# Moving the exponentials one turn later and the squares amid the next unit's scores, in a fused attention and spectral kernel

## The chip, the cores and the metric

The kernel runs on one core of a Trainium2 chip. The core has five engines that work in parallel, each through its own stream of instructions and in order: TensorE (PE, matrix products; its weight loads are listed apart as PEld), VectorE (DVE), ScalarE (ACT), GpSimd (POOL), and SyncE (SP), which here issues the transfers (DMAs). Matrix products read from the on-chip memory SBUF and write to PSUM, which has eight banks of 128 partitions by 512 float32. The metric is the device time of one execution in microseconds, the median of several runs.

## The reference

Two layers, each with a residual, on x of shape (2, 48, 48, 768), all in float32:

```python
qkv = (x.reshape(B, S, dim) @ qkv_w + qkv_b).reshape(B, S, 3, nh, hd)   # S = 2304, 12 heads of 64
...
attn = jnp.einsum('bqc,bkc->bqk', q * scale, k)
rel_h = jnp.einsum('bhwc,hkc->bhwk', r_q, Rh)
rel_w = jnp.einsum('bhwc,wkc->bhwk', r_q, Rw)
attn = (attn.reshape(B * nh, h, w, h, w) + rel_h[:, :, :, :, None] + rel_w[:, :, :, None, :]).reshape(B * nh, S, S)
attn = jax.nn.softmax(attn, axis=-1)
out = (attn @ v).reshape(B, nh, h, w, hd)
...
x = x + attention(_gn(x)) @ proj_w + proj_b
x = x + spectral(_gn(x))    # rfft2, two block-diagonal layers of 8 blocks, softshrink, irfft2
```

`_gn` is a group norm over 32 groups. The change lies in the attention alone; the output projection and the spectral layer stay as they are.

## The kernel before

The two images of the batch are done one after the other: attention, output projection, spectral layer. The normalized input stands transposed in SBUF (`xnT`, channels on the partitions). Attention goes through the heads in 6 pairs, a pair through 6 groups of 8 image rows (384 queries), a group through 3 units of 128 queries (x = 0, 1, 2). So there are 108 units for each image, `order[n]` = (pair, group, x), and one pass of the loop over n (line 502) is a turn.

The work on one unit of two heads:

- `new_unit` (L346): POOL adds the unit's two relative terms from `rhw` into `s`, two operations of 128 x 2304. `s` has four buffers.
- `scores` (L360): ten PE products, five pieces of keys by two heads, into the PSUM banks `ps_s`; DVE adds each to `s` and takes its maximum into `mx`; one reduction makes `nm`, the negated maximum.
- `numerators` (L389): four ACT exponentials, in place in `s`, two halves by two heads, with the sums in `parts`.
- `squares` (L403): DVE transposes `s` in 32 x 32 squares, in place, two operations for each half.
- `exchange` (L409): moves the squares between partitions into `pT`, so that keys stand on the partitions: for each half two ACT copies and six transfers on SP's queue. `pT` has two buffers.
- `weigh` (L423): 36 pairs of PE products of `pT` with the values, into the one bank `ps_o`.
- `finish` (L440): ACT copies `ps_o` to `res`, DVE adds up `parts` into `dens`; after x = 2 SP writes `res` to DRAM (`oT`). `inverses` (L458) takes the reciprocal of six units' sums, which PE transposes (`turn`) and SP writes to `inv_d` in three transfers (`send`).

Beside the units, a turn has one piece of projection work that fills PE: with x = 2 the queries of the group after next (`queries`), otherwise one sixth of the next pair's keys or values (`keys`, `values`). The last pair has no next one, so only its queries are left there. In turns with x = 0, `relative` (L295) multiplies the queries of a group with the table of relative positions; ACT copies the two banks `ps_r` to `rel`, `write` sends `rel` to a DRAM scratch `t` in a skewed layout (two transfers), and `read` fetches the terms from there into `rhw` (two transfers; a read must wait until its write has landed). `load_w` (L194) loads a weight block for the next pair; keys and values share one buffer.

The order of each engine is the order in which the code emits its instructions: PE, DVE, ACT and SP are wrapped in `InOrder`. Evictions of projection banks are put into the lists `by_act` and `by_dve` and emitted by `evict` at a fixed place in the turn. The PSUM banks other than `ps_o` are seven, handed out in turn to `ps_s`, `ps_proj`, `ps_v`, `ps_r` and `ps_i`, so a product waits until the bank seven places earlier has been emptied.

A turn emits, for unit n (`un`), n-1 (`last`) and n-2 (`older`), in this order: scores(un), numerators(un), projection work and weight loads, turn, weigh(older), relative, the ACT evictions, squares and exchange of half 1 of last, write, squares and exchange of half 0 of un, the DVE evictions, read, finish(older), new_unit for n+1, send. In the last turns of an image the functions of `Projection` are called too (`late`): `step` loads the projection weights and the first attention outputs and inverses, and `fill` emits the first output products.

Of the kernel before, what the change touches and what calls it, by code (L numbers as in the profile page):

```python
# [17 lines left out]
P = 128  # L18
# [144 lines left out]
def attention(tc, k, x_b, a, oT, inv_d, late, span, ps_b, ps_o):  # L163
# [12 lines left out]
    with ExitStack() as ctx:  # L176
# [65 lines left out]
        def evict(waiting):  # L242
            while waiting:
                waiting.pop(0)()
# [50 lines left out]
        def relative(g, qT):  # L295

            row0 = min(32, 40 - 8 * g)  # L300
            both = [bank(f"ps_r{h}") for h in range(2)]
            for x in range(3):
                for h in range(2):
                    r = slice(h * HD, (h + 1) * HD)
                    rows = k.rel[r, row0 : row0 + RW]
                    step = REL + 32 - 16 * x - row0
                    pe.matmul(
                        both[h][:, x * 2 * RW : (x + 1) * 2 * RW],
                        lhsT=qT[r, x, :],
                        rhs=bass.AP(rows.tensor, rows.offset, [rows.ap[0], [step, 2], [1, RW]]),  # L310
                        start=True,
                        stop=True,
                    )
            for h in range(2):
                dst = rel[:, :, :, h, :].rearrange("p k x j -> p x k j")
                src = both[h][:, :ROW].rearrange("p (x k j) -> p x k j", x=3, k=2)
                by_act.append(lambda dst=dst, src=src: act.copy(dst, src))

            rhw = qp.tile([P, 3, 2, 2 * HW], F32, tag="rhw", name="rhw")
            t_ds = []  # L320

            def write():
                for kind in range(2):
                    t_d = dp.tile([P * RS + 16], F32, tag=f"t{kind}", name=f"t{kind}")
                    t_ds.append(t_d)
# [17 lines left out]

            return rhw, write, read
# [11 lines left out]
            return {"pr": pr, "g": g, "x": x, "qT": qT, "s": s}  # L356

        PIECES = [(k0, min(S, k0 + 512)) for k0 in range(0, S, 512)]

        def scores(un):  # L360

            mx = smallp.tile([P, 2, len(PIECES)], F32, tag="mx", name="mx")
            for j, (k0, k1) in enumerate(PIECES):
                both = [bank(f"ps_s{h}") for h in range(2)]
                for h in range(2):
                    r = slice(h * HD, (h + 1) * HD)
                    pe.matmul(
                        both[h][:, : k1 - k0],
                        lhsT=un["qT"][r, un["x"], :],
                        rhs=kTs[un["pr"]][r, k0:k1],  # L370
                        start=True,
                        stop=True,
                    )
                for h in range(2):
                    s = un["s"][:, h, k0:k1]
                    dve.tensor_tensor_reduce(
                        out=s,
                        in0=both[h][:, : k1 - k0],
                        in1=s,
                        scale=1.0,  # L380
                        scalar=LOWEST,
                        op0=ALU.add,
                        op1=ALU.max,
                        accum_out=mx[:, h, j : j + 1],
                    )
            un["nm"] = smallp.tile([P, 2], F32, tag="nm", name="nm")
            dve.tensor_reduce(un["nm"], mx, AX.X, ALU.max, negate=True)

        def numerators(un):  # L389

            un["parts"] = smallp.tile([P, 2, 2], F32, tag="parts", name="parts")
            for half in range(2):
                for h in range(2):
                    s = un["s"][:, h, half * 2 * KQ : (half + 1) * 2 * KQ]
                    act.activation(
                        s,
                        s,
                        AF.Exp,
                        bias=un["nm"][:, h : h + 1],
                        accum_out=un["parts"][:, h, half : half + 1],  # L400
                    )

        def squares(un, half):  # L403

# [35 lines left out]
        def finish(un):  # L440

            pr, g, x = un["pr"], un["g"], un["x"]
            if x == 0:
                outs[pr, g] = outp.tile([P, 8, 3, 16], F32, tag="res", name="res")
                if g % 3 == 0:
                    dens[pr, g // 3] = outp.tile([P, 3, 2, 3], F32, tag="dens", name="dens")
            res = outs[pr, g]
            act.copy(res[:, :, x, :], un["o"][:, :P].rearrange("p (y d) -> p y d", d=16))
            dve.tensor_reduce(
                dens[pr, g // 3][:, x, :, g % 3], un["parts"], AX.X, ALU.add  # L450
            )
            if x == 2:
                sync.dma_start(
                    out=oT[pr * P : (pr + 1) * P, g * UQ : (g + 1) * UQ],
                    in_=res.rearrange("p y x d -> p (y x d)"),
                )
# [40 lines left out]
        weights[2] = load_w(2, 0)  # L497
        staged = ((0, 1), queries(0, 1))
        evict(by_act)
        recent = []  # L500
        last = turn = send = None
        for n in range(len(order) + 3):
            un = older = None
            if n < len(order):
                un = ahead
                pr, g, x = order[n]
                if g == 4 and x == 0 and pr + 1 < NP:
                    weights[0] = load_w(0, pr + 1)
                scores(un)
                recent.append(un)  # L510
            write = read = None
            if un is not None:
                numerators(un)
                ready, staged = staged, None
                if x == 2:
                    if n + 4 < len(order):
                        key = order[n + 4][:2]
                        staged = (key, queries(*key))
                    if g == 2 and pr + 1 < NP:
                        weights[2] = load_w(2, pr + 1)  # L520
                    if g == 5 and pr + 2 < NP:
                        weights[1] = load_w(1, pr + 2)
                elif n < 2:
                    for i in range(3):
                        values(0, 3 * n + i)
                    if n:
                        weights[1] = load_w(1, 1)
                elif pr + 1 < NP:
                    i = 2 * g + x
                    for j in range(0 if n == 3 else i, i + 1):  # L530
                        (keys if j < 6 else values)(pr + 1, j % 6)
            if turn is not None:
                turn()
                turn = None
            if n >= len(order) - 1 and recent:
                late(n - len(order) + 2)
            if n > 1 and recent:
                older = recent.pop(0)
                weigh(older)
            if un is not None and ready is not None:  # L540
                key, qT = ready
                rhw, write, read = relative(key[1], qT)
                groups[key] = (qT, rhw)
            evict(by_act)
            if last is not None:
                squares(last, 1)
                exchange(last, 1)
            if write is not None:
                write()
            if un is not None:  # L550
                squares(un, 0)
                exchange(un, 0)
            evict(by_dve)
            if read is not None:
                read()
            if older is not None:
                finish(older)
            if un is not None and n + 1 < len(order):
                ahead = new_unit(*order[n + 1])
            if send is not None:  # L560
                send()
                send = None
            if older is not None and older["x"] == 2 and older["g"] % 3 == 2:
                turn, send = inverses(older["pr"], older["g"] // 3)
            if len(order) - 6 <= n <= len(order):
                late()
            last = un


def shifts(t):  # L570
# [660 lines left out]
```

## Time and profile before

| | |
|---|---|
| median of 3 runs | 3735.52 us (3732.65 to 3735.68) |
| profiled execution | 3736.53 us, its span 3734.3 us |
| PE busy | 3558.8 us, 95% |
| DVE busy | 2914.9 us, 78% |
| ACT busy | 2544.2 us, 68% |
| POOL busy | 2046.2 us, 55% |
| transfers on SP's queue | 601.69 MB, 69.0% of the 16 transfer engines' time |

The profile is of one execution. The span runs from the first to the last instruction; busy times are shares of it. A line of the costliest groups reads: source line, engine, operation, output <- input with shapes, count | busy us, mean ns of one | idle us of the engine just before them and what ended most of it. Most of the attention's operations carry L68, the line of the helper that records them, and are told apart by their tiles. In a timeline or a chain a line begins with the start in us, followed by the duration.

The profile in 40 slices shows the stages: twice some 14 slices of attention with PE full, each followed by the output projection and the spectral layer with DVE and ACT at 2 to 4 tenths:

```profile
PE   8999999999999888989989999999999998879899
DVE  4799998989999983347657999989998999933476
ACT  3788888888888882133237888888888888821432
```

### The profile page before, as it was taken

How to read it: one execution, taken by the hardware profiler on the slowest of the kernel's cores; microseconds unless marked ns; L12 is line 12 of the kernel's file. 1: busy time of each engine (PE TensorE's matmuls, PEld its weight loads, DVE VectorE, ACT ScalarE, POOL GpSimd, SP SyncE). 2: the span in 40 equal slices, each digit the busy share in tenths (PEclk: the TensorE clock that was granted, in tenths of full speed). 3: DMA queues.
4: the chain of work that ended last, by engine and by line, in shares of the span. 5: the costliest groups of instructions: out<-in, count | busy, mean ns of one | idle time of the engine just before them, and what ended most of it. 6: DMA issues, size and time to landing. Idle time of an engine off the chain costs nothing.

```text
span 3734.3 us, 92576 instructions
## 1 busy us (share of the span) xinstructions
PE 3558.8 (95%) x36032; PEld 2485.7 (67%) x36032; DVE 2914.9 (78%) x6788; ACT 2544.2 (68%) x3740; POOL 2046.2 (55%) x662
## 2 busy tenths in 40 slices
PE   8999999999999888989989999999999998879899
PEld 5677776767767655566566777767677676545665
DVE  4799998989999983347657999989998999933476
ACT  3788888888888882133237888888888888821432
POOL 2566757576766663413225667575757666644232
PEclk9999999999999998999989999999999999989999
DMA  3687777778787888634526877777787778886434
GB/s 103 151 181 170 178 174 174 177 167 184 169 180 168 177 190 189 170 95 120 163 77 151 181 171 176 176 172 178 168 184 168 179 169 181 196 188 160 103 112 137
DMA packets 497859, 607.61 MB, mean 163 GB/s; under 512 B 180493, under 2 KB 312973, under 8 KB 497422
## 3 DMA queue, kind: packets, MB, share of 16 engines
q1 hardware_dynamic: 497422, 601.69, 69.0%
q8 instruction: 286, 4.69, 0.6%
q14 instruction: 151, 1.24, 0.1%
HBM read 131.61 MB, written 87.67 MB: 59 GB/s over the span
## 4 chain that ended last, share of the span: by engine, by line
PE 82%; DVE 6%; DMA 4%; ACT 4%; issue 2%; POOL 1%; SPq 1%; ACTq 0%; DVEq 0%; POOLq 0%
PE ps_o L68 21%; PE ps_s L68 20%; PE ps_proj L68 14%; PE acc L68 8%; PE ps_v L68 7%; DVE s L68 3%; PE ps L967 2%; PE ps_u L1002 2%; PE ps_y L727 2%; PE ps_r L68 2%; DMA pT<-s 2%; PE ps_x L1020 1%; SPq L68 1%; ACT pT L68 1%; PE ps_z L907 1%
## 5 line engine op out<-in xcount | busy, mean ns | idle before, releaser
L350 POOL TENSOR_TENSOR s<-rhw 128x2304 f32<-128x2304 f32 x432 | 1740.2, 4061 | 1066.8 <-DMA pT<-s 639.7
L68 DVE CUSTOM_DVE_ANT_0 s<-ps_s,s 128x512 f32<-128x512 f32 (+1 forms) x2160 | 1222.3, 633 | 312.3 <-issue 182.1
L68 ACT ACTIVATE s<-s,nm 128x1152 f32<-128x1152 f32 x864 | 1074.6, 1245 | 346.2 <-DVE nm L68 332.4
L68 DVE STREAM_TRANSPOSE s<-s 128x1152 f32<-128x1152 f32 x864 | 1111.9, 1344 | 5.5 <-ACT s L68 5.5
L68 ACT COPY pT<-s 32x1152 f32<-32x1152 f32 x864 | 993.4, 1150 | 21.7 <-PE ps_o L68 3.9
L68 PE MATMUL ps_o<-pT,v 128*64 128x128 f32 x15552 | 909.7, 277 | 65.1 <-ACT res L68 32.5
L68 PEld LDWEIGHTS ps_o<-pT,v 128*64 128x64 f32 x15552 | 877.8, 139 | 111.9 <-ACT res L68 55.8
L68 PE MATMUL ps_s<-kT,qT 64*128 64x512 f32 (+1 forms) x4320 | 899.0, 555 | 4.4 <-DVE mx L68 3.8
L68 PEld LDWEIGHTS ps_s<-kT,qT 64*128 64x128 f32 x4320 | 430.3, 187 | 418.9 <-issue 350.9
L68 PE MATMUL ps_proj<-xnT,w 128*64 128x384 f32 (+1 forms) x4032 | 589.6, 446 | 2.3 <-ACT gn_rstd L151 2.3
L68 PEld LDWEIGHTS ps_proj<-xnT,w 128*64 128x64 f32 x4032 | 280.8, 137 | 274.7 <-issue 216.9
L748 DVE TENSOR_TENSOR x<-acc,x 32x384 f32<-32x384 f32 (+2 forms) x216 | 119.2, 553 | 277.5 <-PE acc L68 194.7
L68 PE MATMUL acc<-proj 128*128 128x384 f32 x864 | 288.4, 493 | 40.8 <-POOL proj L68 40.8
L68 PE MATMUL ps_v<-w,xnT 128*64 128x128 f32 x5184 | 301.3, 276 | 0.0
L68 PEld LDWEIGHTS ps_v<-w,xnT 128*64 128x64 f32 x5184 | 285.9, 138 | 21.5 <-DVE mx L68 21.5
L68 PEld LDWEIGHTS acc<-proj 128*128 128x128 f32 x864 | 166.1, 193 | 157.5 <-POOL proj L68 41.6
L734 ACT COPY y<-ps_y 112x384 f32<-112x384 f32 x96 | 45.9, 478 | 265.8 <-PE ps_y L727 264.6
L68 POOL TENSOR_TENSOR proj<-proj 128x2304 f32<-128x2304 f32 x12 | 60.6, 5047 | 219.1 <-DMA proj<-inv_d 180.7
L68 DVE DVE_READ_ACCUMULATOR2_ANT mx<- 128x1 f32 x2160 | 179.4, 83 | 0.0
L984 POOL TENSOR_TENSOR spectrum<-spectrum 128x480 f32<-128x480 f32 x80 | 96.2, 1202 | 119.1 <-DVE spectrum L983 90.6
L68 ACT ACTIVATION_READ_ACCUMULATOR s<-s,nm 128x1 f32 x864 | 161.2, 187 | 0.0
L967 PE MATMUL ps<-w,spectrum 96*64 96x96 f32 x3200 | 143.1, 248 | 0.0
(106 smaller groups left out, 2107.1 us busy)
## 6 DMA issues: line engine op xcount, KB each, us to landing
pT<-s SPq DMA_DIRECT2D x2592, 144.0 KB
t<-rel SPq DMA_DIRECT2D x144, 189.0 KB
rhw<-t SPq DMA_DIRECT2D x144, 144.0 KB
y<-y_d SPq DMA_DIRECT2D x40, 360.0 KB
u_d<-spectrum SPq DMA_DIRECT2D x40, 360.0 KB
u<-u_d SPq DMA_DIRECT2D x48, 300.0 KB
xt<-in_x SPq DMA_DIRECT2D x12, 1152.0 KB
w<-in_qkv_w SPq DMA_DIRECT2D x36, 384.0 KB
```

The source lines that it names most:

```text
L68: return lambda *args, **kw: self.tc.keep_in_program_order(op(*args, **kw))
L350: nc.gpsimd.tensor_tensor(s[:, h, :].rearrange("p (y x) -> p y x", x=HW), rhw[:, x, h, :HW][:, :, None].to_broadcast([P, HW, HW]), rhw[:, ...
L727: nc.tensor.matmul(ps[:YP, : 2 * SC], lhsT=k.fw, rhs=part[:, t0 : t0 + 2, ch], start=True, stop=True,)
L734: nc.scalar.copy(y1[:, :, ch], ps[:YP, : 2 * SC].rearrange("p (t c) -> p t c", c=SC))
L748: nc.vector.tensor_tensor(dst, acc[p : p + n, :UQ], dst, ALU.add)
L907: nc.tensor.matmul(ps[:BS, w * 96 : (w + 1) * 96], lhsT=self.y2[s, j][:, w, i * BS : (i + 1) * BS], rhs=k.fh, start=True, stop=True,)
L967: nc.tensor.matmul(ps[64 * r : 64 * r + 64, w * BS : (w + 1) * BS], lhsT=self.o1[:, ri, f0 : f0 + 64], rhs=w2[:, (0, 2, 1, 0)[2 * r + ri], ...
L984: nc.gpsimd.tensor_tensor(val, val, clip, ALU.subtract)
L1002: nc.tensor.matmul(ps[: 2 * HW, :480], lhsT=k.ih, rhs=d2[:, c0 : c0 + 480], start=True, stop=True)
L1020: nc.tensor.matmul(ps[: 2 * HW, : 2 * SC], lhsT=k.iw, rhs=self.u2[s, i][:, t : t + 2, :], start=True, stop=True,)
```

## The change

- `relative` no longer puts the two copies of `ps_r` into the list of ACT evictions; `write` emits them itself, ahead of its two transfers.
- `scores` takes a list of pieces. It is called twice in a turn: for the pieces 0 to 2 (`EARLY`), and for 3 and 4 (`REST`), after which `nm` is reduced.
- `numerators` takes a half. The exponentials of a unit are emitted in the next turn, half 0 and half 1 ahead of that turn's scores, with `finish` between them. `finish` now takes unit n-3 (`weighed`), one turn later than before; its sum of `parts` goes into the list of DVE evictions.
- The squares and the exchange of both halves of unit n-1 stand together between the EARLY and the REST scores of unit n. Before, half 0 came in the unit's own turn and half 1 in the next, both after the scores.
- `write` and `read` stand one after the other at the head of the turn after `relative`, and weight loads at the head of their turn, ahead of everything else on SP's queue. Before, write stood ahead of one half's exchange and read behind it.
- The load of the second pair's key weights moves from turn 1 to turn 2. After the loop the last `turn`, ACT eviction and `send` are emitted once more.

So the new order of a turn is: weight loads, write, read, numerators(last, 0), finish(weighed), numerators(last, 1), scores(un, EARLY), squares and exchange of last for both halves, scores(un, REST), projection work, turn, weigh(older), relative, ACT evictions, DVE evictions, new_unit, send. The operations, their shapes and their number stay the same. The core of the diff:

```diff
-            for h in range(2):
-                dst = rel[:, :, :, h, :].rearrange("p k x j -> p x k j")
-                src = both[h][:, :ROW].rearrange("p (x k j) -> p x k j", x=3, k=2)
-                by_act.append(lambda dst=dst, src=src: act.copy(dst, src))
-
...
             def write():
+                for h in range(2):
+                    act.copy(
+                        rel[:, :, :, h, :].rearrange("p k x j -> p x k j"),
+                        both[h][:, :ROW].rearrange("p (x k j) -> p x k j", x=3, k=2),
+                    )
                 for kind in range(2):
...
-        def scores(un):
-
-            mx = smallp.tile([P, 2, len(PIECES)], F32, tag="mx", name="mx")
-            for j, (k0, k1) in enumerate(PIECES):
+        EARLY, REST = (0, 1, 2), (3, 4)
+
+        def scores(un, pieces):
+
+            if pieces[0] == 0:
+                un["mx"] = smallp.tile([P, 2, len(PIECES)], F32, tag="mx", name="mx")
+            mx = un["mx"]
+            for j in pieces:
+                k0, k1 = PIECES[j]
                 both = [bank(f"ps_s{h}") for h in range(2)]
...
-        def numerators(un):
+        def numerators(un, half):
...
-            dve.tensor_reduce(
+            by_dve.append(lambda: dve.tensor_reduce(
                 dens[pr, g // 3][:, x, :, g % 3], un["parts"], AX.X, ALU.add
-            )
+            ))
...
+            un, last, older, weighed = (units.get(n - i) for i in range(4))
+            if n < N:
+                un = units[n] = ahead
                 pr, g, x = order[n]
                 if g == 4 and x == 0 and pr + 1 < NP:
                     weights[0] = load_w(0, pr + 1)
-                scores(un)
-                recent.append(un)
-            write = read = None
+                if x == 2 and g == 2 and pr + 1 < NP:
+                    weights[2] = load_w(2, pr + 1)
+                if x == 2 and g == 5 and pr + 2 < NP:
+                    weights[1] = load_w(1, pr + 2)
+                if n == 2:
+                    weights[1] = load_w(1, 1)
+            if write is not None:
+                write()
+                read()
+                write = read = None
+            if last is not None:
+                numerators(last, 0)
+            if weighed is not None:
+                finish(weighed)
+            if last is not None:
+                numerators(last, 1)
             if un is not None:
-                numerators(un)
+                scores(un, EARLY)
+            if last is not None:
+                for half in range(2):
+                    squares(last, half)
+                    exchange(last, half)
+            if un is not None:
+                scores(un, REST)
                 ready, staged = staged, None
...
             evict(by_act)
-            if last is not None:
-                squares(last, 1)
-                exchange(last, 1)
-            if write is not None:
-                write()
-            if un is not None:
-                squares(un, 0)
-                exchange(un, 0)
             evict(by_dve)
-            if read is not None:
-                read()
-            if older is not None:
-                finish(older)
...
+        turn()
+        evict(by_act)
+        send()
```

More of the change, by code (lines that the diff above doesn't have):

```diff
@@ L385, in scores @@
                     )
-            un["nm"] = smallp.tile([P, 2], F32, tag="nm", name="nm")
-            dve.tensor_reduce(un["nm"], mx, AX.X, ALU.max, negate=True)
-        def numerators(un):
[L391 to L400, printed above, removed]
-                    )
+            if pieces[-1] == len(PIECES) - 1:
+                un["nm"] = smallp.tile([P, 2], F32, tag="nm", name="nm")
+                dve.tensor_reduce(un["nm"], mx, AX.X, ALU.max, negate=True)
+        def numerators(un, half):
+            if half == 0:
+                un["parts"] = smallp.tile([P, 2, 2], F32, tag="parts", name="parts")
+            for h in range(2):
+                s = un["s"][:, h, half * 2 * KQ : (half + 1) * 2 * KQ]
+                act.activation(
+                    s,
+                    s,
+                    AF.Exp,
+                    bias=un["nm"][:, h : h + 1],
+                    accum_out=un["parts"][:, h, half : half + 1],
+                )
         def squares(un, half):
@@ L448, in finish @@
             act.copy(res[:, :, x, :], un["o"][:, :P].rearrange("p (y d) -> p y d", d=16))
-            dve.tensor_reduce(
+            by_dve.append(lambda: dve.tensor_reduce(
                 dens[pr, g // 3][:, x, :, g % 3], un["parts"], AX.X, ALU.add
-            )
+            ))
             if x == 2:
@@ L499, in attention @@
         evict(by_act)
[L500 to L505, printed above, removed]
+        N = len(order)
+        units = {}
+        ready = turn = send = write = read = None
+        for n in range(N + 3):
+            un, last, older, weighed = (units.get(n - i) for i in range(4))
+            if n < N:
+                un = units[n] = ahead
                 pr, g, x = order[n]
@@ L508, in attention @@
                     weights[0] = load_w(0, pr + 1)
-                scores(un)
-                recent.append(un)
-            write = read = None
-            if un is not None:
-                numerators(un)
+                if x == 2 and g == 2 and pr + 1 < NP:
[14 more added lines that the diff above has]
+                numerators(last, 1)
+            if un is not None:
+                scores(un, EARLY)
[5 more added lines that the diff above has]
+                scores(un, REST)
                 ready, staged = staged, None
                 if x == 2:
-                    if n + 4 < len(order):
+                    if n + 4 < N:
                         key = order[n + 4][:2]
                         staged = (key, queries(*key))
[L519 to L522, printed above, removed]
                 elif n < 2:
@@ L525, in attention @@
                         values(0, 3 * n + i)
-                    if n:
-                        weights[1] = load_w(1, 1)
                 elif pr + 1 < NP:
@@ L534, in attention @@
                 turn = None
[L535 to L538, printed above, removed]
+            if N - 1 <= n < N + 2:
+                late(n - N + 2)
+            if older is not None:
                 weigh(older)
@@ L544, in attention @@
             evict(by_act)
-            if last is not None:
-                squares(last, 1)
-                exchange(last, 1)
-            if write is not None:
-                write()
-            if un is not None:
-                squares(un, 0)
-                exchange(un, 0)
-            evict(by_dve)
-            if read is not None:
-                read()
-            if older is not None:
-                finish(older)
-            if un is not None and n + 1 < len(order):
+            evict(by_dve)
+            if n + 1 < N:
                 ahead = new_unit(*order[n + 1])
@@ L562, in attention @@
                 send = None
-            if older is not None and older["x"] == 2 and older["g"] % 3 == 2:
-                turn, send = inverses(older["pr"], older["g"] // 3)
-            if len(order) - 6 <= n <= len(order):
+            if weighed is not None and weighed["x"] == 2 and weighed["g"] % 3 == 2:
+                turn, send = inverses(weighed["pr"], weighed["g"] // 3)
+            if N - 6 <= n <= N:
                 late()
-            last = un
+        turn()
+        evict(by_act)
+        send()
 def shifts(t):
```

## The prediction, written before the changed kernel ran

> **What bounds the kernel now.** I read first the busy time of each engine by stretch, because the averages of the page (PE 95%) mix stages. Columns: stretch, its length, PE, PEld, DVE, ACT, POOL busy, granted PE clock, DMA share, GB/s.
>
> ```profile
> 186.00:1186.00 1000.00, 1000.00 (x11445) 718.09 (x11441) 904.64 (x2147) 856.13 (x1173) 652.58 (x162) 1.00 0.78 175
> 1205.00:1399.40 194.40, 164.41 (x1636) 116.99 (x1632) 174.06 (x415) 164.34 (x223) 130.29 (x33) 0.94 0.82 180
> 1399.40:1484.00 84.60, 66.58 (x435) 44.34 (x436) 33.16 (x67) 24.07 (x35) 24.30 (x10) 0.86 0.81 183
> ```
>
> The first line is the attention of five head pairs, the main stretch: PE never stands still, so no reordering on other engines can shorten it, it can only lengthen it. The second is the last pair, which has no next pair's projections to fill PE: 30.0 us of PE idle. The third is the drain after it: 18.0 us idle. Batch 1 repeats all three (idle 31.1 us in 3062 to 3270, 24.3 us in 3270 to 3346). Next, who let PE wait, in the whole run:
>
> ```profile
> PE acc L68 <- POOL proj L68: 40.8, 2, 23.1
> PE ps_o L68 <- ACT res L68: 32.5, 15, 2.9
> PE ps_o L68 <- DMA pT<-s: 30.5, 13, 6.0
> ```
>
> The same view limited to 186 to 1186 is empty: these waits lie in the last pairs and drains. Starts of successive nm reductions give the turn: 12.3 us in the main stretch (by x 12.7, 12.05, 12.15), and 207.4 and 205.0 us for the 17 intervals of the two last pairs, 12.2 and 12.1 each, though several intervals are 10.88 (DVE back to back).
>
> Then the durations, and the queue of SP in one main turn and at the very start:
>
> ```profile
> L68 DVE CUSTOM_DVE_ANT_0 s<-ps_s,s 128x512 f32<-128x512 f32 (+1 forms) x2160 | 1222.3, 633 | 312.3 <-issue 182.1
> L68 ACT ACTIVATE s<-s,nm 128x1152 f32<-128x1152 f32 x864 | 1074.6, 1245 | 346.2 <-DVE nm L68 332.4
> L68 DVE STREAM_TRANSPOSE s<-s 128x1152 f32<-128x1152 f32 x864 | 1111.9, 1344 | 5.5 <-ACT s L68 5.5
> L68 ACT COPY pT<-s 32x1152 f32<-32x1152 f32 x864 | 993.4, 1150 | 21.7 <-PE ps_o L68 3.9
> ```
>
> ```profile
> 801.78 3.88 SPq L68 DMA_DIRECT2D pT<-s  x6
> 805.95 1.35 SPq L68 DMA_DIRECT2D t<-rel  x2
> 807.47 5.50 SPq L68 DMA_DIRECT2D pT<-s  x6
> 813.02 1.27 SPq L68 DMA_DIRECT2D rhw<-t  x2
> ```
>
> ```profile
> 59.38 1.42 SPq L68 DMA_DIRECT2D t<-rel  x2
> 62.88 1.47 SPq L68 DMA_DIRECT2D rhw<-t  x2
> ```
>
> Today six pT transfers stand between the write of t and its read, and cover its landing. At the start nothing does: from first write to end of reads SP is held 64.35 - 59.38 = 4.97 us. That is the order which the change makes in every group.
>
> **The change, part by part, in the main stretch.** Time 0 is a turn's first score matmul. PE: scores to 4.07, projection to 8.15, weigh to 12.2; then ps_r, 0.94, if x is 0.
>
> *Both squares amid the scores.* DVE's first addition starts 1.2 us after PE's first score (816.79 to 818.05). Six at a 0.613 spacing end at 4.9, four squares (5.15 in the timeline) at 10.05, four additions (2 x 0.61 + 2 x 0.35) and nm at 12.2; the next turn's first addition is due at about 13.2. So 1 us of DVE is spare, 0.5 where a v eviction follows. If that cover were gone, each 0.1 us would cost 180 turns x 0.1 = 18 us. PSUM: the projection reuses the bank of the fourth addition, free at 3.65, wanted at 4.07, as today. The second ps_r bank is emptied at 1.15 of the next turn and wanted at 2.7, the first at 0.75 against 1.8. Cost 0.
>
> *Exponentials a turn later.* ACT: the copies that follow the second half's squares end at 12.45, a kT eviction (0.56) at 13.0, that is 1.0 of the next turn; the rel copies (0.85, one turn in three) to 1.2 or, if the eviction is late, 1.85; four exponentials at 1.24 with the res copy (0.27) end at 6.3 to 7.1. DVE wants the last half at 7.47. Cost 0, spare 0.4 to 1.2.
>
> *Twelve pT transfers in one stretch.* The first issue is at 7.55, and a spacing of 0.64 ends the issues at 15.25. Where SP issued twelve in a row today (from 826.49), the trace's landing records have the last at 837.24, 10.75 us later; so 18.3. weigh of that unit stands at 12.0 + 8.15 = 20.1 or later. Cost 0, spare 1.8.
>
> *Relative terms first.* In the turn with x = 1, SP is free of the previous issues at 2.5. Write and read hold it 4.97 if alone; behind the older transfers (landing to 5.5) the second t lands about 7.9 (two t after a last pT took 2.6 us at 844.94 to 847.53), and the reads end at 8.4. Behind them wait twelve pT, then the weigh: last landing 8.4 + 10.75 = 19.15 against 20.1. Spare 0.95, cost 0. But in 2 groups of each pair the three inv_d issues (2.4 us at 797.25) stand just ahead: reads end at about 9.8, landing 20.55, weigh 0.45 late. 5 pairs x 2 x 2 batches = 20 groups, **+9 us**. Bounds: 0 if t lands 0.5 us sooner, and +43 if it lands 1.2 us later (20 x 1.65 + 40 x 0.25).
>
> [...]
>
> *Weight loads first:* three per pair, 0.38 us of SP each (66.40). Their buffers were read last in the turn before, so they don't wait; the load's use is a turn or more later. In turn 2 SP no longer waits for the values ahead of an exchange (16.4 us in two waits today), which PE doesn't feel. POOL gets rhw at about 11 of the turn with x = 1, today at 13.8 (818.64 against 804.88), so its sums are earlier. The den reduction (0.12) moves inside DVE's spare. Start-up: PE works through its projections, 0.
>
> **Last pair.** The res copy no longer stands behind squares and four pT copies, so the wait of 32.5 us on ACT res goes. What is late next is the transfer: from a unit's first addition D, half 0's squares end at 6.25, the twelfth landing is at 17.0, weigh 4.15, then the next-but-one unit's scores and its first addition (1.2): 22.4 us for two turns, 11.2 each, with DVE's floor at 10.88. Where ps_r follows the weigh, +0.94; where the read holds SP (normally 6.33, here about 8.0), +1.9. One group of three turns is half of 6 turns: (22.4 + 0.94) + (22.4 + 1.9) + 22.4 = 70.0, so 35.0. Today's groups: 36.1, 35.3, 35.8, 37.4, 39.8, then 23.0 for the two last intervals. I take 35.0 for three, 36.5 for the two in which projection loads share the queue, 22.3: 200.3 against 207.4, **-7 a batch, -14 in all**. Bounds: 0 (the loop eats the gain) and 17 x (12.15 - 10.88) = 21.6 a batch, -43.
>
> **Drain.** The chain of waits:
>
> ```profile
> 1426.25 7.96 DMA proj<-inv_d
> ...
> 1434.43 5.04 POOL proj L68
> ...
> 1439.52 7.08 PE acc L68 x12
> 1446.60 4.08 PE ps_o L68 x72
> ```
>
> The inv_d read that the product waits for is issued behind the last unit's first six pT, which wait for its exponentials. Afterwards only the older unit's twelve stand ahead: D = 1406.8, squares 1413.1, issues to 1420.8 instead of 1426.25, 5.5 us earlier; the queue of transfers already backed up (inv_d of 1413.44 landed at 1422.82) gives back about 1. **-4.5 a batch, -9.** Bounds 0 and -11 (the full 5.5).
>
> **Sum.** +9 - 14 - 9 = -14. Profiled execution 3736.5 (span 3734.3 and 2.2 around it) gives 3722.5; the median shown, 3735.5, is 1.0 below that execution: **3721.5**.
>
> **Rivals.** *The read holds the queue too long* (slower): if t lands later than I count by e, the 20 groups lose 0.45 + e each and the 40 others e - 0.95. The break-even is where this equals 23: e = 0.7. At e = 1.2 it is +43, and net 3735.5 + 43 - 23 = 3755.5. For: the DMA share is 0.78 and rhw landings vary from 3.1 to 5.9 us after issue. Against: the landings taken are already loaded ones. *No change:* in the last pair the two-turn loop is no shorter than today's (squares of half 1 at D + 8.35, six transfers landed 8.06 later in the chain at 1195.72 to 1203.78, 4.15, 1.2: 21.8) and gives back what ACT frees, and +9 meets -9: 3735.5. For: several intervals today are 10.88, under my 11.2. Against: the ACT res waits are real. *DVE's floor:* no transfer wait remains in the last pair and none arises before: -43 - 9, 3683.5. That the change doesn't do what it says, because an engine's order stays as it was, is excluded by the explicit program order on PE, DVE, ACT and SP.
>
> **How the numbers follow.** Forecast 0.44, slower rival 0.28, no change 0.20, DVE's floor 0.08. This kernel is told from no change at about 0.2%, 7.5 us: under 3728 or over 3743. The forecast's own range is 3710 to 3731, with 0.04 of its 0.44 above 3728; the no-change case spills 0.02 to the faster side: faster 0.40 + 0.08 + 0.02 = 0.50, same 0.04 + 0.18 = 0.22, slower 0.28. Range 3700 to 3760: it cuts the floor case and the slower case beyond +48 before the gains.
>
> **What would show it.** Right: the main stretch still has PE at 100% or within 0.5%, with a few waits of ps_o on pT under 1 us in turns with x = 2; ACT res is gone from PE's waits; last pairs near 200 us; POOL's first proj 4 to 5 us sooner after the last nm's turn begins. Wrong: ps_o waiting for pT in every group, a main turn over 12.4, or waits of scores for DVE (mx) in the main stretch, which would say that DVE's 1 us isn't there.

## The result and the profile after

| | before | after |
|---|---|---|
| median | 3734.09 us (3731.14 to 3735.68, 4 runs) | 3907.16 us (3901.48 to 3913.89, 4 runs) |
| profiled span | 3734.3 us | 3903.7 us |
| PE busy | 3558.8 us | 3623.9 us |

The ratio is 1.0465, 95% interval 1.0446 to 1.0484: the change makes the kernel 4.65% slower. The forecast was 3721.5 us in a range of 3700 to 3760.

Where the 169 us of span sit follows from the first score product of each unit, taken from both traces: +1.4 in the start, +25 in the first pair of the two images, **+110 in the pairs 2 to 5** (1771.9 to 1882.3 us, both images), +32 in the last pair of the two, +0.6 in what follows the attention. The main stretch, which the forecast held to be nearly untouched, carries most of it. The busy time of the same stretch (columns as before):

```profile
186.00:1186.00 1000.00, 957.74 (x10616) 684.07 (x10614) 847.14 (x2017) 795.05 (x1098) 617.28 (x153) 0.98 0.72 164
```

PE now stands still for 42 of 1000 us, and its granted clock is 0.98 instead of 1.00. Who lets it wait, in the whole run:

```profile
PE ps_o L68 <- DMA pT<-s: 110.5, 45, 3.8
PE ps_o L68 <- DMA oT<-res: 41.1, 19, 10.4
PE acc L68 <- POOL proj L68: 30.7, 2, 18.5
...
PE ps_s L68 <- DVE mx L68: 6.3, 7, 1.6
```

The wait for ACT's res copy (32.5 us before) is no longer in the list, DVE is late for 6.3 us in all, and the weigh waits for its transfers 110.5 us instead of 30.5. The second line names oT, but in the turns with x = 2 of the pairs 2 to 5 it is the same wait: each late weigh began 0.1 to 0.5 us after its last pT landed, and the copy that empties `ps_o` had ended over 5 us before.

Turn by turn (mean over 8 turns each, pairs 2 to 5 of both images) the turns with x = 0 and x = 1 keep their length within 0.4 us. All the loss is in the turns with x = 2, whose weigh takes the unit that was exchanged in the turn with x = 1:

| turns with x = 2, us, by group g | 0 | 1 | 2 | 3 | 4 | 5 |
|---|---|---|---|---|---|---|
| before, without the product of `turn` in 0 and 3 | 12.02 | 12.02 | 12.05 | 12.02 | 12.02 | 12.05 |
| after | 12.45 | 14.91 | 16.84 | 12.48 | 14.71 | 14.56 |

(That product, 0.36 us, stood in the groups 0 and 3 before and stands in x = 0 of 1 and 4 now.) Times 8 turns the excess makes 58 us in groups 2 and 5, 45 in 1 and 4, 7 in 0 and 3: 110 in all. SP's queue of the changed kernel tells these groups apart. An ordinary one:

```profile
813.68 1.31 SPq L68 DMA_DIRECT2D t<-rel  x2
817.62 1.41 SPq L68 DMA_DIRECT2D rhw<-t  x2
819.20 7.81 SPq L68 DMA_DIRECT2D pT<-s  x12
```

Group 1, then group 2 of a pair:

```profile
379.65 2.37 SPq L68 DMA_DIRECT2D inv_d<-turned  x3
382.12 1.32 SPq L68 DMA_DIRECT2D t<-rel  x2
385.55 1.49 SPq L68 DMA_DIRECT2D rhw<-t  x2
387.21 8.15 SPq L68 DMA_DIRECT2D pT<-s  x12
...
418.85 1.31 SPq L68 DMA_DIRECT2D t<-rel  x2
423.46 0.38 SPq L197 DMA_DIRECT2D w<-in_qkv_w  x1
423.94 1.08 SPq L68 DMA_DIRECT2D rhw<-t  x2
425.12 9.20 SPq L68 DMA_DIRECT2D pT<-s  x12
```

In group 1 the three inv_d issues stand ahead, as the forecast said. In group 2 a weight load (L197) stands **between the write and the read**, a turn earlier than the code emits it: `load_w` issues through `nc.sync` and not through the wrapper that keeps an engine's order, so the scheduler was free to put it there. PE's products of that time show what the load waits for:

```profile
419.32 4.09 PE L68 MATMUL ps_proj<-xnT,w 128*64 128x384 f32 x24
423.25 4.10 PE L68 MATMUL ps_o<-pT,v 128*64 128x128 f32 x72
427.28 4.14 PE L68 MATMUL ps_s<-kT,qT 64*128 64x512 f32 x20
431.34 4.12 PE L68 MATMUL ps_proj<-xnT,w 128*64 128x192 f32 x48
438.44 7.08 PE L68 MATMUL ps_o<-pT,v 128*64 128x128 f32 x72 [2.98 <-DMA pT<-s]
```

The load overwrites the weights that the projection at 419.32 still reads; SP issues it at 423.46, when that projection has ended, and read and twelve pT follow. The weigh at 438.44 waits 2.98 us for the last pT and then takes 7.08 instead of 4.10 us, because PE's clock fell while it waited: the granted clock is 1.00 from 430 to 437 us, 0.73 from 437 to 438.4 and 0.58 from 438.4 to 445.6. The slower clock is a good part of the loss: PE's busy time rose by 65 us for the same instructions, at a mean granted clock of 0.964 instead of 0.978, which leaves about 104 of the 169 us for waiting.

### The profile page after: what moved, and what is told of

The parts are those of the page before. It is cut to its first block, busy times and chain, and to the rows that moved or that the text cites. A ratio compares the mean times of both kernels' runs of the same rounds, so it can differ in the third digit from the quotient of the medians.

```text
span 3903.7 us, 92806 instructions
## 1 busy us (share of the span) xinstructions
PE 3623.9 (93%) x36032; PEld 2537.2 (65%) x36032; DVE 2917.3 (75%) x6788; ACT 2527.0 (65%) x3740; POOL 2050.3 (53%) x662
## 4 chain that ended last, share of the span: by engine, by line
PE 60%; DMA 13%; DVE 12%; SPq 7%; ACT 3%; issue 3%; POOL 2%; ACTq 0%; POOLq 0%; DVEq 0%
PE ps_o L68 16%; PE ps_s L68 12%; DVE s L68 9%; PE ps_proj L68 8%; SPq L68 7%; PE acc L68 7%; PE ps_v L68 6%; DMA pT<-s 6%; DMA t<-rel 2%; PE ps L975 2%; PE ps_u L1010 2%; DMA rhw<-t 2%; PE ps_y L735 1%; ACT s L68 1%; PE ps_x L1028 1%
## 5 line engine op out<-in xcount | busy, mean ns | idle before, releaser
L68 PE MATMUL ps_o<-pT,v 128*64 128x128 f32 x15552 | 959.6, 286 | 175.9 <-DMA pT<-s 110.5
L68 PEld LDWEIGHTS ps_o<-pT,v 128*64 128x64 f32 x15552 | 923.5, 145 | 239.7 <-issue 175.0
```

The costliest lines, as they stand in the source:

```text
L68: return lambda *args, **kw: self.tc.keep_in_program_order(op(*args, **kw))
```

## The experiments

Theory A after the result: twelve pT transfers now lie between a unit's squares and its weigh, where before half 0's six had a turn more; whatever else stands on SP in the turn with x = 1 eats their small spare. In order of price these are the load, the inv_d issues, and the write and read of t. The rival B differs by run. A time that has no interval beside it is a single execution; the kernel before ranged from 3727 to 3742 us over its executions. The turns with x = 2 in the six groups, and the times:

| kernel | us | 0 | 1 | 2 | 3 | 4 | 5 |
|---|---|---|---|---|---|---|---|
| loads in order | 3832.89 | 12.60 | 14.63 | 12.36 | 12.75 | 14.61 | 12.66 |
| inv_d behind the exchanges | 3838.57 | 12.66 | 12.17 | 16.35 | 12.61 | 12.42 | 14.81 |
| read amid the pT | 3826.36 | 12.81 | 13.07 | 13.36 | 12.99 | 13.46 | 13.71 |
| all three | 3822.63 | 13.01 | 12.78 | 13.61 | 13.03 | 13.18 | 13.93 |
| loads and inv_d | 3778.43 | 12.63 | 12.18 | 12.36 | 12.47 | 12.46 | 12.73 |
| the same, t not written nor read | 3738.3 | 12.02 | 12.02 | 12.05 | 12.02 | 12.02 | 12.08 |

**The loads in order.** From the changed kernel:

```diff
-            nc.sync.dma_start(
+            sync.dma_start(
                 out=w,
```

> Only the weight loads change: they are kept in the written order on SP's queue, at the head of the turn with x = 2, instead of between the write of t and its read one turn earlier. Theory A (SP's queue is held by the load's wait for the projection's last product): the turns with x = 2 of groups 2 and 5, today 16.8 and 14.6 us against 12.05 before, fall under 12.6; with 5 and 4 loads per image that is 2 x (5 x 4.8 + 4 x 2.5) = 68 us, so about 3840 us. Theory B (the moved exponentials and squares themselves slow the turn; the queue is a bystander): under 10 us gained, 3900 us. Theory C (the read directly behind the write holds the queue whatever the load does): half of it at most, over 3870 us.

3832.89 us, as A has it. The groups 2 and 5 fall from 16.84 and 14.56 to 12.36 and 12.66, the others stay within 0.3: the load alone cost 74 us.

**The inv_d transfers behind the next turn's exchanges.**

```diff
                     exchange(last, half)
+            if send is not None and turn is None:
+                send()
+                send = None
...
-            if send is not None:
-                send()
-                send = None
```

> Only the three inv_d transfers move: behind the pT transfers of the next turn instead of directly ahead of the write of t. Theory A: turns with x = 2 of groups 1 and 4, today 14.9 and 14.7 us against 12.02 before, fall to about 12.5; 2.8 us x 2 groups x 5 pairs x 2 images = 56, and some 10 in the last pairs, so about 3840 us; groups 2 and 5 stay. Theory B: no gain, 3900 us.

3838.57 us, as A has it. Only the groups 1 and 4 recover: 69 us in the whole run.

**The read behind the first six pT.**

```diff
                 write()
-                read()
-                write = read = None
+                write = None
...
                     exchange(last, half)
+                    if half == 0 and read is not None:
+                        read()
+                        read = None
```

> Only the read of t moves: behind the first six pT transfers instead of directly behind the write. Theory A: SP no longer stands waiting for t, the inv_d groups lose their excess, the weight groups most of theirs (the load then stands between write and the first pT or later), about 3770 us. Theory B: no gain, 3900 us. Theory C (the read is the cause, the load alone isn't): all groups under 12.6 us.

3826.36 us, which none of the three theories has. It frees the stalled groups (the load now stands in the turn with x = 2, ahead of oT), but every group is now 0.8 to 1.7 us late, the ordinary ones too.

**All three together.**

> The three edits together; exponentials, squares and finish stay where the change put them. Theory A: the main stretch is back at 12.3 us a turn, the last pair at or below the 207 us of before, the drain unchanged: 3735 us, plus 10 or minus 25. Theory B: over 3850 us.

3822.63 us (1.0217 of the kernel before, interval 1.0188 to 1.0245): far from A, and no better than the read amid the pT alone. So the read amid the transfers is harmful by itself. That called for the next two.

**Loads and inv_d without the read's move.**

> The changed kernel with the two repairs that helped alone (the weight loads held to the head of their turn, the inv_d transfers behind the exchanges of the next turn), the read left directly behind the write. Theory A (the two causes sit in different groups and add; the read apart was harmful by itself): 3907 less 74 less 69 = 3764, so 3750 to 3780 us, with the turns of x = 2 between 12.2 and 12.7 in every group. Theory B (the three were one cause, the queue's total): about 3822 as with all three.

3778.43 us (1.0124, interval 1.0105 to 1.0144): within A's 3750 to 3780. The two causes add. What is left is 39 us of span: 22 in the pairs 2 to 5, 15 in the last pair of the two images, 2 elsewhere. In the last pair another load still stands ahead of pT: the projection's weights (L606) are also issued through `nc.sync`, and in this kernel as in the changed one, in one turn with x = 1 of each image, two of them stand directly ahead of the write of t and one between write and read. No run held those.

**The same without the way of t through DRAM.** `relative` returns the first group's `rhw`, and a write that makes only its ACT copies:

```diff
...
+            if rhws:
+                return rhws[0], copies(both), lambda: None
...
```

> The same, but in the loop the relative terms are not written to DRAM and not read back: every unit uses those of the first group, so the output is not the reference's; all matmuls, evictions and copies stay. It leaves the twelve pT transfers alone on the queue between a unit's exponentials and its product. Theory A (what is left of the loss in the pairs 2 to 5 is the write and read of t standing ahead of pT in the same turn): turns of x = 2 at 12.0 to 12.1 as before, 20 to 40 us less than the kernel with the two repairs. Theory B (twelve pT due in one turn are late by themselves): every turn, those with x = 0 and x = 1 too, stays as with the two repairs, within 10 us of it.

3738.3 us, and the main stretch is full again:

```profile
186.00:1186.00 1000.00, 1000.00 (x11401) 716.59 (x11399) 904.88 (x2152) 848.25 (x1175) 656.68 (x163) 1.00 0.67 157
```

So the twelve pT alone meet their deadline, DVE's and ACT's spare holds, and in the pairs 2 to 5 the write and read of t were the whole rest. The time itself can't be told from that of the kernel before.

**Is it the read's place, or the deadline behind it?** In the kernel before, the read put directly behind the write; and once more with the loads held in order:

```diff
             if write is not None:
                 write()
+                read()
...
-            if read is not None:
-                read()
```

> The kernel before, with one step of the change alone: t's read stands directly behind its write, ahead of the six transfers of the next unit's half 0; exponentials, squares, finish and loads stay. Theory A (a read is harmful only where the transfers behind it fall due in the next turn, and here half 0's six have a whole turn more): 3725 to 3745 us, turns with x = 2 stay at 12.0 to 12.1 us and ps_o waits for pT no more than now (30 us). Theory B (a read that holds SP for 3 to 4 us shifts everything behind it, whatever the deadline): about 0.45 us a group and more, 3760 us or over.

> The kernel before with the read directly behind the write, as in the run that cost 95 us, and the weight loads held to the place in which the code issues them. Theory A (all of those 95 us came from the load that the scheduler put between write and read, where it holds SP until PE has read the old weights; the read's place by itself costs nothing there, where half 0 has a turn to spare): 3725 to 3745 us, turns of x = 2 in the groups 2 and 5 at 12.1 instead of 16.5. Theory B (the read's place is a loss in those groups by itself): 3790 us or over.

The first took 3829.54 us: the time is B's and not A's, but the place is neither's. No x = 2 turn grew by over 0.11 us but those of the groups 2 and 5, to 16.52 and 16.18. SP's queue of that run shows why:

```profile
412.07 1.31 SPq L68 DMA_DIRECT2D t<-rel  x2
418.28 0.38 SPq L197 DMA_DIRECT2D w<-in_qkv_w  x1
418.77 1.07 SPq L68 DMA_DIRECT2D rhw<-t  x2
419.94 12.83 SPq L68 DMA_DIRECT2D pT<-s  x18
```

The load had again been put between write and read. With the loads held it stands behind the exchanges and oT, and the run took 3740.52 us, as A has it, within the range of the kernel before and with all x = 2 turns as before within 0.04. The same order of write and read that costs 22 us in the main stretch of the changed kernel costs nothing that can be told where half 0's six pT have a turn more. That fits the deadline as what decides, and not the place by itself.

**The read behind all twelve pT** (loads and inv_d repaired as above):

```diff
...
+            if read is not None and write is None:
+                read()
+                read = None
...
```

> The changed kernel with the weight loads held to the head of their turn, the inv_d transfers behind the next turn's exchanges, and t's read behind all twelve pT of the turn in which t is written. Theory A (twelve pT in one turn meet their deadline when nothing else stands ahead of them; the write of t alone, 1.3 us on SP, is covered): turns of x = 2 at 12.0 to 12.2 in every group, the pairs 2 to 5 within 5 us of the kernel before (886 an image), 3730 to 3750 us in all. Theory B (the read hurts wherever it stands in that turn, as it did behind the first six, since the relative terms come late for the next group or its transfers share the engines): 3775 us or over.

4005.57 us (1.0719, interval 1.0701 to 1.0737), the slowest of all: the time is B's. The x = 2 turns are right (12.02 to 12.12), but those with x = 0 grew to 16 to 18 us. SP, POOL and PE of that run:

```profile
386.24 1.31 SPq L68 DMA_DIRECT2D t<-rel  x2
391.58 8.93 SPq L68 DMA_DIRECT2D pT<-s  x12
400.56 1.26 SPq L68 DMA_DIRECT2D rhw<-t  x2
```

```profile
404.93 24.14 POOL L350 TENSOR_TENSOR s<-rhw 128x2304 f32<-128x2304 f32 x6 [17.68 <-DMA inv_d<-turned]
```

```profile
408.49 3.70 PE L68 MATMUL ps_s<-kT,qT 64*128 64x512 f32 x16
413.79 1.59 PE L68 MATMUL ps_s<-kT,qT 64*128 64x256 f32 x4 [1.60 <-DVE mx L68]
415.31 5.45 PE L68 MATMUL ps_proj<-xnT,w 128*64 128x384 f32 x24
```

```profile
413.04 0.69 DVE L68 CUSTOM_DVE_ANT_0 s<-ps_s,s 128x512 f32<-128x512 f32 x1 [2.60 <-POOL s L350]
```

The read issued at 400.56 has landed at 404.7; POOL, idle for 17.68 us, starts then and needs 8.1 us for the next group's first unit, whose scores begin at 408.49. They wait for DVE's additions, and DVE waits for POOL until 413.04. So the read has a deadline of its own, and it lies before the end of the twelve pT.

**The read from POOL's queue** (loads and inv_d repaired):

```diff
...
-                    sync.dma_start(
+                    (nc.gpsimd if ring else sync).dma_start(
...
```

(`ring` is empty for the first group alone, whose read stays on SP.)

> The changed kernel with the loads held and the inv_d transfers behind the exchanges (3778 us), and with the read of t issued from POOL's queue instead of SP's, so that the read's wait for t no longer stands ahead of the twelve pT; its transfers are the same ones and move at about the same time. Theory A (what is left of the loss is SP being held while t lands): 3735 to 3755 us, turns of x = 2 at 12.0 to 12.2. Theory B (it is the transfers of t and rhw among the pT, or POOL's own additions wait for the issue): 3765 us or over.

3869.55 us: the time is B's. The x = 2 turns took 13.2 to 14.3:

```profile
379.93 0.85 POOL L337 DMA_DIRECT2D rhw<-t  x1 [3.54 <-DMA t<-rel]
384.49 0.83 POOL L337 DMA_DIRECT2D rhw<-t  x1 [3.71 <-DMA pT<-s]
392.56 24.15 POOL L352 TENSOR_TENSOR s<-rhw 128x2304 f32<-128x2304 f32 x6 [7.24 <-DMA inv_d<-turned]
```

SP was free and issued the first pT on time, but POOL's second read began 4.6 us after the first, and the transfers of both moved amid the pT. A table of the turn with x = 1 sets the runs side by side: medians over 48 turns (pairs 2 to 5, both images), us from the turn's first score product, from issue and completion events in the traces. "Weigh due" is when PE is done with what stands ahead of the weigh that needs these twelve.

| kernel | first pT issued | last pT landed | from one to the other | weigh due |
|---|---|---|---|---|
| t not written nor read | 7.60 | 18.53 | 10.90 | 20.12 |
| loads and inv_d | 8.72 | 19.99 | 11.18 | 20.13 |
| after | 9.76 | 21.75 | 11.24 | 20.13 |
| read amid the pT | 7.60 | 20.82 | 13.22 | 20.12 |
| read on POOL's queue | 7.60 | 21.09 | 13.49 | 20.12 |

Alone, the twelve have 1.6 us to spare. The read ahead of them takes 1.1 by holding SP and 0.3 more after that. Amid them it takes 2.3 on SP's queue, of which 1.5 is SP's time (its issues of pT end at 17.2 instead of 15.7), and 2.6 on POOL's queue, where SP's issues end only 0.3 later and the rest is in the transfers.

**The relative products earlier** (behind the early scores of x = 0, the write behind that turn's pT, the read at the head of the next; loads and inv_d repaired):

```diff
...
                 scores(un, EARLY)
+                ready, staged = staged, None
+                if ready is not None:
+                    key, qT = ready
+                    rhw, copies, write, read_next = relative(key[1], qT)
+                    groups[key] = (qT, rhw)
+                    copies()
...
```

> The changed kernel with the loads held and the inv_d transfers behind the exchanges (3778 us), and with the relative terms computed earlier: their products stand behind the early scores of the turn with x = 0, ACT copies them there, SP writes t behind that turn's twelve pT and reads it back at the head of the next turn, before that turn's pT are due. Theory A (the read must come before the twelve pT for POOL and the twelve pT must not wait for it; a write one turn earlier satisfies both): turns of x = 2 at 12.0 to 12.2, as with the relative terms left out, 3730 to 3750 us. Theory B (the earlier products take PSUM banks and ACT time amid the scores, and DVE or the exponentials become late): 3760 us or over, with the loss in the turns with x = 0.

3788.18 us (1.0147, interval 1.013 to 1.0164): the time is B's, and 10 us more than without the earlier products. SP issues the pT of the turn with x = 0 until 3 us into the next turn, so t came only 0.4 us sooner (median 3.0 instead of 3.4), the x = 2 turns took 12.05 to 12.60, and those with x = 0 grew by 0.24, those with x = 1 by 0.1; the runs don't show what made these longer.

**The finish one turn later, alone, in the kernel before:**

```diff
...
+            done = [weighed] if weighed is not None else []
+            for u in done:
+                finish(u)
+            weighed = None
             if un is not None:
                 numerators(un)
...
```

> The kernel before, with one step of the change alone: a unit's finish (the copy of its result out of ps_o, and its sum) stands a turn later, ahead of the next exponentials, as in the changed kernel, and in the drain where it was. Theory A (the wait of ps_o for the copy of res, 32.5 us in 15 places, is on the path in part): 3705 to 3730 us, the wait gone from the list. Theory B (these waits give way to others behind them, as the product is 4 us and the next scores wait for the same ACT): 3730 to 3745 us.

3734.52 us, ratio 0.9996 (interval 0.9987 to 1.0006): no difference that can be told, and the wait is still there:

```profile
PE ps_o L68 <- ACT res L68: 37.1, 16, 2.9
```

So the later finish alone doesn't take the wait away. None of the twelve kernels beat the kernel before.

## Why the prediction was wrong, point by point

**What bounds the main stretch: right.** It was PE-bound and could only get longer; even with t left out the changed order gains nothing there (1772.0 us in the pairs 2 to 5, 1771.9 before).

**Squares, exponentials, twelve pT: right.** Waits for DVE are 6.3 us in the whole run, ACT res is gone, and the last of twelve pT lands 10.90 us after the first issue where the text had 10.75. The spare of 1.8 was 1.6.

**Weight loads first: this is the step that failed most.** "Their buffers were read last in the turn before, so they don't wait" took the place in the code for the place on the queue. The load isn't bound to it; it was built in a turn early, where its buffer was still being read, and held SP ahead of the read and the twelve pT. It was counted at 0 and cost 74 us. The text's sentence that the program order is explicit on SP was wrong for the loads that go through `nc.sync`: these of `load_w`, and in the last pair the projection's weights. The line of L197 in the profile before, behind oT, could not show it, since a new order gave the scheduler a new place.

**Relative terms first: the mechanism right, the sizes wrong.** The 20 groups behind inv_d were named, at 0.45 us each, 9 us; the 16 of them that lie in the pairs 2 to 5 cost 45, and putting inv_d later saved 69 in the whole run. Their turns are 2.7 to 2.9 us longer, more than the text's upper bound of 1.65, and part of that is the slower clock after the wait: 5 of their 16 weighs took 5.82 to 7.08 instead of 4.10 us. In the other groups the text had the reads ended at 8.4 and the last landing at 19.15, a spare of 0.95. With loads and inv_d out of the way the first pT is issued at 8.72 and the last lands at 19.99 in the median: 0.14 to spare, so that 22 of 48 turns miss it, for 22 us in the pairs 2 to 5. Two terms were short: SP is free of the older pT at 3.3 and not at 2.5 (the issues end at 16.1 of a 12.85 us turn, not at 15.25), of which 0.3 is left at the first pT, and twelve pT behind a read take 11.18 in the median and not 10.75. The rival "the read holds the queue too long" came nearest: the twelve land 0.84 late (19.99 less 19.15), but little of that is a late t, since the reads end at 8.54 where the text had 8.4. Its price of 3755.5 lacked the load and the clock. From the first write's issue to the first read's, SP took 3.7 us in the median with loads and inv_d repaired (3.37 to 7.06 of the turn), where the row at the start had 3.5 (59.38 to 62.88).

**The price of a wait.** The sum counted a late weigh as its lateness. The clock adds to it, as the last section shows, and the trace of the kernel before already had it: in its last pairs and drains, after 2.4 to 2.9 us of idle PE, 9 of 12 weighs took 5.5 to 7.1 us where the text's sum for the last pair has 4.15.

**Last pair: -14 forecast, +32 measured,** +3 with t left out. Before, PE's waits of ps_o there were, within 1180 to 1440 us:

```profile
PE ps_o L68 <- ACT res L68: 16.0, 7, 2.9
PE ps_o L68 <- DMA pT<-s: 15.3, 7, 6.0
```

and in the run without t, over the same window:

```profile
PE ps_o L68 <- DMA pT<-s: 20.3, 9, 2.9
...
PE ps_o L68 <- DMA proj<-in_proj_w: 5.1, 1, 5.1
```

The res wait went, and the wait for pT and for the late loads took its place, as the rival "no change" had it for this stretch. That accounts for the missing gain; of the 32, 15 are left with loads and inv_d repaired and 3 with t left out as well, and what share the projection's loads have is not shown.

**Drain: -9 forecast, about 0 kept.** The gain is real where it was put: from the last unit's first score, the first output product comes 5.5 and 4.0 us sooner in the two images (28.5 and 28.7 instead of 34.0 and 32.6). In the first image it is given back at once. The chain of waits of the changed kernel:

```profile
1538.00 4.11 PE ps_o L68 x72
...
1545.29 9.02 DMA x<-in_x
...
1558.67 6.79 PE acc L68 x12
```

The load of x comes behind the last inv_d issues, and the products that in the kernel before ran on without a break wait for it. In the second image the gain lasts to the end of the products and has shrunk to 1.2 us by the end of the run.

## What to carry to other kernels

Before moving a stage later, count what its successor's transfers have left between issue and need, and everything else that the same queue holds in that stretch; here 1.6 us of spare met a read of 1.4, three small writes of 2.4 and a load that waits. An instruction that is not bound to its place is part of a change even if nobody moved it: look where it stands in the built order. And a transfer with a deadline on either side (here the read, wanted by POOL before, and in the way of PE's operand after) can make every order of one queue that was tried a loss. The one attempt to get the room from an earlier stage gained 0.4 us of start and no time; whether more room there would do is not shown.

## What the runs showed of the hardware that was not expected

PE's granted clock fell to 0.5 at weighs that came after 2.0 to 3.7 us of idle PE, though not at every one. For the changed kernel's main stretches (186 to 1186 and 2100 to 3100 us) the 72 products of a weigh took, by PE's idle time before them:

| idle before | weighs | min, median, max us | over 5 us |
|---|---|---|---|
| under 0.3 us | 110 | 4.10, 4.10, 4.15 | 0 |
| 0.3 to 2 us | 16 | 4.15, 4.15, 4.15 | 0 |
| 2 to 2.5 us | 6 | 4.15, 5.79, 5.82 | 5 |
| 2.5 to 3 us | 16 | 4.15, 5.79, 7.08 | 9 |
| 3 to 4 us | 4 | 5.70, 6.82, 7.08 | 4 |

The granted clock in the same trace stands at 0.5 eighteen times in these two stretches, for 3.41 or 6.83 us, each time at one of the 18 slow weighs and at no other. A wait of 2.0 to 3.0 us thus cost, where the clock fell, mostly some 1.7 us more in the weigh alone (5.82 instead of 4.10 us). It fell in 14 of the 22 cases with such a wait; what tells them from the other 8 is not shown.

And the two transfers of the read, each of as many bytes as one pT (128 x 288 numbers against 32 x 1152) but in rows of 48 numbers, delay the last pT by 2.6 us when they move amid them from POOL's queue, with SP's issues only 0.3 later, but by 1.4 when they go ahead with SP held for them: here it was cheaper to keep the queue waiting than to let such a read share it.
